# First images of both halves: the second skip and the transform along w one cycle later, and half 0's output banks emptied by two engines

## The chip, the core and the metric

The kernel runs on one core of a Trainium2 chip. The core has five engines with queues of their own, each in order: PE (TensorE, matrix products), DVE (VectorE), ACT (ScalarE), POOL (GpSimd) and SP (SyncE, which only issues DMAs here). POOL and ACT issue DMAs too. Matmul results go to PSUM, eight banks of 128 partitions x 512 fp32. The metric is device time in microseconds of one execution: 2630.17 before the change, the median of three runs (2627.25 to 2636.5).

## The reference, cut to what matters

Two layers work on an image x of 256 x 256 points with 128 channels. Layer 0 is a gated attention along the rows, added to x. Layer 1 is a spectral block on the 256 images (tokens) of 256 x 128 points into which its input is cut. Its last part, to which the change belongs, reads in the reference:

```python
h0 = instance_norm(attn, norm2_w, norm2_b)
h1 = fno_layer(h0, mix_wr[0], mix_wi[0], ..., norm=True, act=True)
h2 = fno_layer(h1, mix_wr[1], mix_wi[1], ..., norm=True)
out = instance_norm(h2, mon_w, mon_b) + attn
```

An fno_layer adds a "skip" (a product with a 4 x 4 matrix over groups of four channels) to a spectral convolution (Fourier modes, mixed, and turned back into an image), the latter normed; the first of the two has a GELU behind it.

## The kernel before, in words

All times below are microseconds from the start of the span. Layer 0 ends at about 1450. Layer 1 handles its 256 tokens as two halves of 128 (one token per partition), half 0 and half 1, each image in 16 blocks of 2048 pixels. h1 of half 0, later of half 1, lies in SBUF in the tile `blocks`; `hb[b]` is its block b. The stages at the end follow each other like this:

1. `first_images(0, ...)`, 1964 to 2098: makes h1 of half 0, block by block, and the Fourier transform of h1 along w, written to `Yd`.
2. 2098 to 2241: the last blocks of y (attn before its norm) of half 1, the second modes of half 0 and the first modes of half 1.
3. `first_images(1, ...)` woven with `output_0`, 2241 to 2440: h1 of half 1 block by block, while half 0's output image h2 is made and written.
4. 2440 to the end: the second modes of half 1 and its output (`LastModes`, `Output1`).

**first_images** (L1695) runs a loop over cycles b = 0 to 16. One cycle of the old code puts on the queues:

- the loads of block b+1 on SP (`load`, L1701: four DMAs of 64 KB for the modes `gs`; in half 1 also two of 512 KB for `y`), and in half 0 the loads of the old image `xw` (`load_w`, L1711, two of 512 KB);
- first skip of block b into four PSUM banks `ups` (L1387, 32x32 tiles of PE, sixteen at a time), then `image` (L1372, tiles of 32x128) into the same banks, then four GELUs on ACT from the banks to `hb[b]` (L1750);
- in half 0, `add_w(b+1)` (L1719): ACT scales the raw block b+1 into the tile `w0` (L1727), POOL adds `xw` to it (L1730) and issues the write to `wd` (L1731). Blocks that were summed in an earlier stage are left out: 0, 1, half of 2, and 9 to 11;
- for block b-1: sixteen transposes on PE into four banks `htps` (L1762), copied to the tiles `hT` by DVE (L1774, and L1765 for the last, which ACT copies in half 1);
- here the loop yields 0, and in half 1 the caller puts in one step of `output_0`;
- for block b-1: second skip into four banks `sps` (L1387), of which DVE takes statistics (`bn_stats`, L1782); the product along w of the four `hT` into one bank `psA` (L1785), copied by ACT to `yA` (L1787) and written to `Yd` by a DMA from POOL's queue (L1788);
- the loop yields 1, and in half 1 the caller puts in the next step of `output_0`.

Buffers that set the order: `ups` (and `h2ps` of output_0) rotate over one set of four banks, `htps`, `sps` and `psA` over another set of four. `hT` has four tiles, `yA` two, `gs` of the first images two, `w0` three. `xw` for the second half of a block has one tile (L1715), so its load for the next block waits until POOL has added it.

**output_0** (L2088) calls `output` (L2072) for each block of half 0. The first step puts a skip (L1387) and an image (L1372) into four banks `h2ps` and has ACT empty all four into `hb[b]` (L2079). The second step has DVE add the result to `w` (L2085) and POOL issue the writes to the output (L2086). Its loads (`wd` 1024 KB at L2094, `gs` 4 x 64 KB) go to SP one block ahead. In half 1, block b's GELUs write over `hb[b]`, which output_0 must have added by then.

The queues of these stages are written out by hand: each engine executes in the order in which the program gives it its instructions.

Of the kernel before, what the change touches and what calls it, by code (L numbers as in the profile page):

```python
# [10 lines left out]
FP = mybir.dt.float32  # L11
AF = mybir.ActivationFunctionType
ALU = mybir.AluOpType
# [5 lines left out]
P = 128  # L19
# [681 lines left out]
def layer1(tc, I, C, ident, x1d, upool, U, Q2, groups, out):  # L701
# [6 lines left out]
    nc = tc.nc  # L708
    NT, H, W = 256, 256, 128
    L = lambda n: I["L1_conv_" + n]  # L710
    with ExitStack() as ctx:
# [86 lines left out]
        wp = gctx.enter_context(tc.tile_pool(name="wp", bufs=3))  # L798
# [35 lines left out]
        with tc.manual_schedule(engines=COMPUTE):  # L834
# [292 lines left out]
            ps = psa.tile([P, 512], FP, tag="a", name="gtps")  # L1127
# [9 lines left out]
            bfwd = load_const(late, "bfwd")  # L1137
# [4 lines left out]
            for t in range(2):  # L1142
                for b in range(2):
                    ps = psa.tile([P, 512], FP, tag="a", name=f"fvps_{t}_{b}")
# [49 lines left out]
        wp = hctx.enter_context(tc.tile_pool(name="wp2", bufs=2))  # L1194
# [86 lines left out]
        with tc.manual_schedule(engines=COMPUTE):  # L1281
# [25 lines left out]
            for sc in range(2):  # L1307
                nc.vector.tensor_scalar(mpT[:, sc, :], mT[:, sc, :], acol[:, sc, 0:1], None, ALU.mult)
                d = mpT[:, sc, sc * P : (sc + 1) * P]
# [5 lines left out]
            ps = psa.tile([P, 512], FP, tag="a", name="mbps")  # L1315
# [20 lines left out]
            for c in range(4):  # L1336
                ps = psa.tile([P, 512], FP, tag="a", name=f"fyps_{c}")
# [20 lines left out]
        hb = [blocks[:, b, :] for b in range(16)]  # L1358

        def by_turn(t):  # L1360

            return t.rearrange("p (n j w) -> p j n w", j=4, w=W)

        def rows_of(ps):
            return ps.rearrange("p (n w) -> p n w", w=W)
# [11 lines left out]
        def skip(ps, src, blk, stop):  # L1377


            parts = src if isinstance(src, list) else [src]  # L1380
            for k, part in enumerate(parts):
                n = slice(k * 4 // len(parts), (k + 1) * 4 // len(parts))
                for j in range(4):
                    for i in range(4):
                        r, o = slice(32 * i, 32 * i + 32), slice(32 * (i ^ j), 32 * (i ^ j) + 32)
                        w = blk[r, r] if len(blk.shape) == 2 else blk[r, j]
                        nc.tensor.matmul(rows_of(ps[j][o, :])[:, n], w, part[r, j], start=(k == 0), stop=stop)  # L1387
# [32 lines left out]
        hstat = sp.tile([P, 64, 6], FP, name="hstat")  # L1420
# [274 lines left out]
        def first_images(a, wp, yp, psk, pst, first=None):  # L1695


            h = halves[a]
            ys, gss = {}, {}

            def load(b):  # L1701
                if a == 1:
                    ys[b] = []
                    for k in (2 * b, 2 * b + 1):
                        pool, tag, bufs = (wp, "wx", 1) if k % 3 == 0 else (yp, "yt", 2)
                        ys[b].append(pool.tile([P, HB], FP, tag=tag, name=f"y2_{k}", bufs=bufs))
                        nc.sync.dma_start(ys[b][-1], ydv[:, a, k * HB : (k + 1) * HB])
                gss[b] = wp.tile([P, 4, P], FP, tag="gs2", name=f"gs2_{a}_{b}")
                load_modes(gss[b], h.Gd1, b)

            def load_w(b):  # L1711
                for s in range(2):
                    if 2 * b + s in h.summed:
                        continue
                    t = (yp, "yt", 2) if s == 0 else (wp, "xw", 1)  # L1715
                    ys[b, s] = t[0].tile([P, HB], FP, tag=t[1], name=f"xw_{b}_{s}", bufs=t[2])
                    nc.sync.dma_start(ys[b, s], x1v[:, a, b * NB + s * HB : b * NB + (s + 1) * HB])

            def add_w(b):  # L1719

                todo = [s for s in range(2) if (b, s) in ys]
                if not todo:
                    return
                t = yp.tile([P, NB], FP, tag="xt", name=f"w0_{b}", bufs=3)
                for s in todo:
                    px = slice(s * HB, (s + 1) * HB)
                    nc.scalar.activation(t[:, px], hb[b][:, px], AF.Identity, scale=h.col[:, 3:4])  # L1727
                for s in todo:
                    px = slice(s * HB, (s + 1) * HB)
                    nc.gpsimd.tensor_tensor(t[:, px], t[:, px], ys.pop((b, s)), ALU.add)  # L1730
                    nc.gpsimd.dma_start(wd[:, b * NB + s * HB : b * NB + (s + 1) * HB], t[:, px])  # L1731

            if first is None:
                load(0)
            else:
                ys[0], gss[0] = first
            if a == 0:
                load_w(0)
                add_w(0)
            for b in range(17):  # L1740
                if b < 15:
                    load(b + 1)
                    if a == 0:
                        load_w(b + 1)
                if b < 16:
                    ps = [psk.tile(f"ups_{a}_{b}_{j}") for j in range(4)]
                    skip(ps, [by_turn(y) for y in ys.pop(b)] if a else by_turn(hb[b]), h.bl0, False)
                    image(ps, gss.pop(b), bs4)
                    for j in range(4):
                        nc.scalar.activation(  # L1750
                            by_turn(hb[b])[:, j], rows_of(ps[j]), AF.Gelu,
                            bias=h.turn[:, 2 * j + 1 : 2 * j + 2], scale=h.turn[:, 2 * j : 2 * j + 1],
                        )
                    if a == 0 and b < 15:
                        add_w(b + 1)
                if b > 0:
                    turned = by_turn(hb[b - 1])
                    hT = {}
                    for j in (1, 2, 3, 0):
                        ps = pst.tile(f"htps_{a}_{b}_{j}")  # L1760
                        for n in range(4):
                            nc.tensor.transpose(ps[:, n * P : (n + 1) * P], turned[:, j, n, :], ident)  # L1762
                        t = hT[j] = wp.tile([P, 512], FP, tag="hT", name=f"hT_{a}_{b}_{j}", bufs=4)
                        if j == 0:
                            (nc.scalar.copy if a else nc.vector.tensor_copy)(t, ps)  # L1765
                            continue
                        v = t.rearrange("p (n c d x) -> p n c d x", n=4, c=2, d=2)
                        if j == 1:
                            v = v[:, :, :, ::-1].rearrange("p n c d x -> p (n c) d x")
                        elif j == 2:  # L1770
                            v = t.rearrange("p (n c x) -> p n c x", n=4, c=2)[:, :, ::-1]
                        else:
                            v = t.rearrange("p (n c x) -> p n c x", n=4, c=4)[:, :, ::-1]
                        nc.vector.tensor_copy(  # L1774
                            v, ps.rearrange("p (m c x) -> p m c x", m=v.shape[1], c=v.shape[2])
                        )
                yield 0
                if b > 0:
                    ps = [pst.tile(f"sps_{a}_{b}_{j}") for j in range(4)]
                    skip(ps, turned, blk[1], True)  # L1780
                    for j in range(4):
                        nc.vector.bn_stats(hstat[:, 4 * (b - 1) + j, :], ps[j])  # L1782
                    psA = pst.tile(f"psA_{a}_{b}")
                    for j in (1, 2, 3, 0):
                        nc.tensor.matmul(psA[32 * j : 32 * j + 32, :], bfwd, hT[j], start=True, stop=True)  # L1785
                    yA = wp.tile([P, 512], FP, tag="yA", name=f"yA_{a}_{b}")
                    nc.scalar.copy(yA, psA)  # L1787
                    (nc.scalar if a and b == 16 else nc.gpsimd).dma_start(  # L1788
                        h.Yd[16 * (b - 1) : 16 * b].rearrange("(n j) f t -> (j f) n t", j=4),
                        yA.rearrange("f (n t) -> f n t", n=4),  # L1790
                    )
                yield 1

        def turned_blocks(h):
# [277 lines left out]
        def output(a, b, gs, w, psk):  # L2072

            krs, c0 = (halves[a].col[:, k : k + 1] for k in (14, 9))
            ps = [psk.tile(f"h2ps_{a}_{b}_{j}") for j in range(4)]
            skip(ps, by_turn(hb[b]), by_blocks(halves[a].bl0), False)
            image(ps, gs, bs4)
            for j in range(4):
                nc.scalar.activation(  # L2079
                    by_turn(hb[b])[:, j], rows_of(ps[j]), AF.Identity, bias=c0, scale=krs  # L2080
                )
            yield
            for s in range(2):
                px = slice(b * NB + s * HB, b * NB + (s + 1) * HB)
                nc.vector.tensor_tensor(w[s], w[s], hb[b][:, s * HB : (s + 1) * HB], ALU.add)  # L2085
                nc.gpsimd.dma_start(outv[:, a, px], w[s])  # L2086
# [307 lines left out]
```

## Time and profile before

| what | value |
|---|---|
| time, median of three runs | 2630.17 us (2627.25 to 2636.5) |
| profiled execution, its own time | 2637.42 us |
| span of that execution | 2635.7 us |
| PE busy in the span | 2418.5 us (92%) |
| DVE, ACT, POOL busy | 2024.6, 1422.7, 1476.0 us |
| first images of half 0, from the first skip to the last psA | 1963.9 to 2098.3 |
| first images of half 1 with output_0, from the first h2ps to yA of block 15 | 2241.2 to 2439.8 |
| GELU from a bank, ACT (L1750), one | 777 ns |
| emptying an h2ps bank, ACT (L2079), one | 776 ns |
| copy of a bank to hT, DVE (L1774), one | 685 ns |
| bn_stats of a bank, DVE (L1782), one | 686 ns |
| add of xw, POOL (L1730), one | 2370 ns |

In a timeline row the first two numbers are the start and the length of a run of like instructions; the ends of matmuls are modelled, and consecutive ones overlap a little, so the distance between two starts is the better measure of PE's time. In a table by windows, the last three columns are PE's granted clock (1.00 is full), the mean busy share of the 16 DMA engines, and what they moved. A busy share a little over 1 means saturated.

### The profile page before, as it was taken

What the parts mean: (1) busy time and instruction counts of PE and PEld (TensorE: products, weight loads), DVE (VectorE), ACT (ScalarE), POOL (GpSimd) and SP (SyncE); (2) the same over time, 40 slices, a digit from 0 to 9 for tenths busy, and PEclk for the clock granted to TensorE, in tenths of its full rate; (3) what the DMA queues carried; (4) which work ended last, traced back from release to release, by engine and by line L of the source; (5) the groups of instructions that cost most, each with busy time, mean ns of one, the idle gap of its engine ahead of it and who ended that gap; (6) DMA issues with size and microseconds to landing.
All of it is one profiled execution on the core that took longest, in us unless ns stands there. A gap on an engine that the chain in (4) does not pass through costs nothing. (4 is left out here: it accounts for less than half of the span.)

```text
span 2635.7 us, 88777 instructions
## 1 busy us (share of the span) xinstructions
PE 2418.5 (92%) x37590; PEld 1546.8 (59%) x37590; DVE 2024.6 (77%) x2872; ACT 1422.7 (54%) x2732; POOL 1476.0 (56%) x1043
## 2 busy tenths in 40 slices
PE   6899999999999999999998999998979978899754
PEld 5555556565556555656554567786754556455633
DVE  7799999999999999999997457567645645465455
ACT  0377888888888888888885122001016401565232
POOL 1299999999999999999995012002136411111011
PEclk9999999999999999999999999999989988899855
DMA  9755565666656565665653011788877764998699
GB/s 364 217 101 102 102 109 103 106 106 108 105 103 108 102 109 102 109 104 105 108 104 65 5 59 65 264 272 291 296 276 260 238 239 140 316 361 312 195 377 349
DMA packets 1016549, 458.49 MB, mean 174 GB/s; under 512 B 831062, under 2 KB 946729, under 8 KB 1009752
## 3 DMA queue, kind: packets, MB, share of 16 engines
q1 hardware_dynamic: 980120, 364.71, 55.0%
q0 software_dynamic: 22832, 81.54, 8.0%
q10 hardware_dynamic: 13200, 6.56, 0.9%
q8 instruction: 298, 4.88, 0.8%
q14 instruction: 99, 0.81, 0.1%
HBM read 317.36 MB, written 135.27 MB: 172 GB/s over the span
## 5 line engine op out<-in xcount | busy, mean ns | idle before, releaser
L422 POOL TENSOR_TENSOR e<-e,b1T 128x1024 f32<-128x1024 f32 x255 | 604.8, 2372 | 82.6 <-ACT e L404 82.0
L427 POOL TENSOR_TENSOR es<-e 128x512 f32<-128x512 f32 x512 | 648.9, 1289 | 0.1
L449 DVE RECIPROCAL av<-av 128x256 f32<-128x256 f32 x256 | 452.2, 1766 | 9.1
L404 ACT ACTIVATE sc<-sc,b2T 128x512 f32<-128x512 f32 x514 | 340.0, 662 | 122.4 <-PE sc L395 109.9
L404 ACT ACTIVATE e<-sc,b2T 128x512 f32<-128x512 f32 x510 | 323.4, 694 | 0.0
L420 DVE TENSOR_TENSOR e<-sc,b1T 128x1024 f32<-128x1024 f32 x257 | 312.3, 1215 | 7.1 <-ACT sc L404 3.6
L395 PE MATMUL sc<-qkT 32*128 32x256 f32 x4096 | 294.9, 401 | 1.2 <-DVE e L420 1.2
L1505 PE MATMUL yps<-xt,mpT 128*128 128x256 f32 x1024 | 249.1, 394 | 30.8 <-DMA xt<-x1d 15.0
L437 PE MATMUL av<-e,v 128*32 128x256 f32 x4096 | 268.7, 379 | 1.8 <-DVE gate L450 1.7
L395 PEld LDWEIGHTS sc<-qkT 32*128 32x128 f32 x4096 | 185.7, 184 | 113.4 <-issue 52.7
L1505 PEld LDWEIGHTS yps<-xt,mpT 128*128 128x128 f32 x1024 | 193.6, 194 | 75.7 <-DVE yt L1517 20.0
L437 PEld LDWEIGHTS av<-e,v 128*32 128x32 f32 x4096 | 130.1, 109 | 125.9 <-issue 38.5
L1521 POOL DMA_DIRECT2D yd<-yt x32 | 17.5, 546 | 324.6 <-DVE yt L1517 322.1
L367 ACT ACTIVATE qkT<-qk,qb 128x512 f32<-128x512 f32 x256 | 174.4, 681 | 3.2 <-PE qk L337 3.2
L337 PE MATMUL qk<-turned,wT_wk 128*32 128x256 f32 x2048 | 164.5, 393 | 0.4 <-DVE g_ve L35 0.4
L494 ACT ACTIVATE turned<-turned 128x256 f32<-128x256 f32 x256 | 104.4, 409 | 111.7 <-DVE x1b L462 109.4
L337 PEld LDWEIGHTS u<-adft,x 128*32 128x32 f32 x4096 | 118.5, 110 | 74.9 <-issue 74.7
L442 PE MATMUL av<-es,ones 128*32 128x256 f32 x2048 | 160.7, 379 | 1.5 <-POOL es L427 1.5
L2079 ACT ACTIVATE blocks<-h2ps,col 128x512 f32<-128x512 f32 x128 | 88.9, 779 | 130.4 <-PE h2ps L1372 130.4
L345 DVE STREAM_TRANSPOSE turned<-xk 128x1024 f32<-128x1024 f32 x128 | 158.1, 1235 | 0.4 <-DMA xk<-in_L_conv_kv_x_dram 0.4
L337 PE MATMUL qk<-turned,wn_wq 128*32 128x256 f32 x2048 | 157.9, 380 | 0.0
L2086 POOL DMA_DIRECT2D out_dram<-w x64 | 34.3, 536 | 186.6 <-DVE w L2085 186.4
(566 smaller groups left out, 4266.0 us busy)
## 6 DMA issues: line engine op xcount, KB each, us to landing
xt<-x1d SPq DMA_DIRECT2D x128, 512.0 KB, 7.2
U<-in_x_dram SPq DMA_DIRECT2D x32, 1024.0 KB, 10.3
xk<-in_x_dram SPq DMA_DIRECT2D x512, 64.0 KB, 3.0
xk<-in_L_conv_kv_x_dram SPq DMA_DIRECT2D x512, 64.0 KB, 2.6
x1d<-x1b SPq DMA_DIRECT2D x512, 64.0 KB, 2.2
out_dram<-w POOLq DMA_DIRECT2D x64, 512.0 KB, 7.9
x<-x1d SPq DMA_DIRECT2D x126, 256.0 KB, 3.4
y<-yd SPq DMA_DIRECT2D x62, 512.0 KB, 8.8
```

The costliest lines, as they stand in the source:

```text
L337: nc.tensor.matmul(out[hd], w[:, hd], src, start=start, stop=stop)
L345: nc.vector.transpose(turned[:, a : b + 1 : b - a].rearrange("p k (b c) -> p k b c", c=32), t)
L367: nc.scalar.activation(r["qkT"], ps, AF.Identity, bias=self.qb)
L395: nc.tensor.matmul(sc[h // 2][:, h % 2, c * 256 : (c + 1) * 256], qkT[p, 256 + c * P : 256 + (c + 1) * P], qkT[p, 0:256], start=True, stop ...
L404: nc.scalar.activation(r["e"][1][:, :, c, :] if hp and s < NS - 1 else z, z, AF.Exp, bias=b2T[:, c, s : s + 1])
L420: nc.vector.tensor_tensor(e, sc.rearrange("p h x -> p (h x)"), w, ALU.mult)
L422: nc.gpsimd.tensor_tensor(e, e, w, ALU.mult)
L427: nc.gpsimd.tensor_tensor(es, e[:, :, 0, :], e[:, :, 1, :], ALU.add)
L437: nc.tensor.matmul(ps[hd, 0:256], p["v"][:, 2 * (s % 2) + c, hd], r["e"][h // 2][:, h % 2, c, :], start=(c == 0), stop=(c == 1),)
L442: nc.tensor.matmul(ps[32 * h : 32 * h + 32, 256:512], self.ones, r["es"][h // 2][:, h % 2, :], start=True, stop=True,)
L449: nc.vector.reciprocal(rd, rd)
L1505: nc.tensor.matmul(rows_of(ps[j]), mpT[:, sc, tt], by_turn(xt[:, sc])[:, j], start=(sc == 0), stop=False,)
```

## The change

The loop of `first_images` goes over 18 cycles in place of 17, and its parts become small functions. Transposes of block b-1 stay in cycle b; the second skip (with its statistics) and the product along w (with its write) handle block b-2.

- In half 0 a cycle now gives PE: first skip of b, second skip of b-2, image of b, product along w of b-2, transposes of b-1. The two skips are one run of 32x32 tiles.
- In half 1 the second skip of b-2 comes first, then the first skip of b. The skip of output_0, put in at the yield, is not next to it in PE's queue: its image lies between.
- ACT's four GELUs are split: banks 0 and 1, then the copy `yA` of block b-2, then banks 2 and 3. In half 0 `add_w(b+1)` comes behind the transposes in program order, so on ACT it still follows the GELUs.
- At the end, the product along w of block 15 comes before the second skip of block 15.
- In `output` of half 0, DVE empties banks 2 and 3 of `h2ps` with a tensor_scalar; ACT empties 0 and 1.
- On POOL's and SP's queues half 0 keeps its order: the write of `Yd` of block b-1 still follows the adds of block b+1. In half 1 the write of `Yd` comes one output block later in POOL's queue.

The core of the diff:

```diff
-            for b in range(17):
+            for b in range(18):
                 if b < 15:
                     load(b + 1)
                     if a == 0:
                         load_w(b + 1)
+                if a and 1 < b < 17:
+                    second_skip(b - 2)
                 if b < 16:
-                    ps = [psk.tile(f"ups_{a}_{b}_{j}") for j in range(4)]
-                    skip(ps, [by_turn(y) for y in ys.pop(b)] if a else by_turn(hb[b]), h.bl0, False)
+                    ps = first_skip(b)
+                if not a and 1 < b < 17:
+                    second_skip(b - 2)
+                if b < 16:
                     image(ps, gss.pop(b), bs4)
...
+                    gelu(b, ps, (0, 1))
+                if b > 1:
+                    along_w(b - 2)
+                if b < 16:
+                    gelu(b, ps, (2, 3))
+                if 0 < b < 17:
+                    turn_back(b - 1)
+                if a == 0 and b < 15:
+                    add_w(b + 1)
                 yield 0
...
+                if b == 17:
+                    second_skip(15)
                 yield 1
...
             for j in range(4):
-                nc.scalar.activation(
-                    by_turn(hb[b])[:, j], rows_of(ps[j]), AF.Identity, bias=c0, scale=krs
-                )
+                if a == 0 and j > 1:
+                    nc.vector.tensor_scalar(by_turn(hb[b])[:, j], rows_of(ps[j]), krs, c0, ALU.mult, ALU.add)
+                else:
+                    nc.scalar.activation(
+                        by_turn(hb[b])[:, j], rows_of(ps[j]), AF.Identity, bias=c0, scale=krs
+                    )
```

`second_skip`, `along_w`, `turn_back`, `first_skip` and `gelu` hold the old statements unchanged, apart from the block index.

More of the change, by code (lines that the diff above doesn't have):

```diff
@@ L1739, in first_images, with turn_back @@
                 add_w(0)
-            for b in range(17):
+            hTs = {}
+            def turn_back(b):
+                turned = by_turn(hb[b])
+                hT = hTs[b] = {}
+                for j in (1, 2, 3, 0):
+                    ps = pst.tile(f"htps_{a}_{b}_{j}")
+                    for n in range(4):
+                        nc.tensor.transpose(ps[:, n * P : (n + 1) * P], turned[:, j, n, :], ident)
+                    t = hT[j] = wp.tile([P, 512], FP, tag="hT", name=f"hT_{a}_{b}_{j}", bufs=4)
+                    if j == 0:
+                        (nc.scalar.copy if a else nc.vector.tensor_copy)(t, ps)
+                        continue
+                    v = t.rearrange("p (n c d x) -> p n c d x", n=4, c=2, d=2)
+                    if j == 1:
+                        v = v[:, :, :, ::-1].rearrange("p n c d x -> p (n c) d x")
+                    elif j == 2:
+                        v = t.rearrange("p (n c x) -> p n c x", n=4, c=2)[:, :, ::-1]
+                    else:
+                        v = t.rearrange("p (n c x) -> p n c x", n=4, c=4)[:, :, ::-1]
+                    nc.vector.tensor_copy(
+                        v, ps.rearrange("p (m c x) -> p m c x", m=v.shape[1], c=v.shape[2])
+                    )
@@ new lines, in second_skip, with along_w @@
+            def second_skip(b):
+                ps = [pst.tile(f"sps_{a}_{b}_{j}") for j in range(4)]
+                skip(ps, by_turn(hb[b]), blk[1], True)
+                for j in range(4):
+                    nc.vector.bn_stats(hstat[:, 4 * b + j, :], ps[j])
+            def along_w(b):
+                hT = hTs.pop(b)
+                psA = pst.tile(f"psA_{a}_{b}")
+                for j in (1, 2, 3, 0):
+                    nc.tensor.matmul(psA[32 * j : 32 * j + 32, :], bfwd, hT[j], start=True, stop=True)
+                yA = wp.tile([P, 512], FP, tag="yA", name=f"yA_{a}_{b}")
+                nc.scalar.copy(yA, psA)
+                (nc.scalar if a and b == 15 else nc.gpsimd).dma_start(
+                    h.Yd[16 * b : 16 * b + 16].rearrange("(n j) f t -> (j f) n t", j=4),
+                    yA.rearrange("f (n t) -> f n t", n=4),
+                )
@@ new lines, in first_skip, with gelu @@
+            def first_skip(b):
+                ps = [psk.tile(f"ups_{a}_{b}_{j}") for j in range(4)]
+                skip(ps, [by_turn(y) for y in ys.pop(b)] if a else by_turn(hb[b]), h.bl0, False)
+                return ps
+            def gelu(b, ps, js):
+                for j in js:
+                    nc.scalar.activation(
+                        by_turn(hb[b])[:, j], rows_of(ps[j]), AF.Gelu,
+                        bias=h.turn[:, 2 * j + 1 : 2 * j + 2], scale=h.turn[:, 2 * j : 2 * j + 1],
+                    )
@@ L1744, in first_images @@
                         load_w(b + 1)
+                if a and 1 < b < 17:
+                    second_skip(b - 2)
                 if b < 16:
-                    ps = [psk.tile(f"ups_{a}_{b}_{j}") for j in range(4)]
-                    skip(ps, [by_turn(y) for y in ys.pop(b)] if a else by_turn(hb[b]), h.bl0, False)
+                    ps = first_skip(b)
+                if not a and 1 < b < 17:
+                    second_skip(b - 2)
+                if b < 16:
                     image(ps, gss.pop(b), bs4)
-                    for j in range(4):
-                        nc.scalar.activation(
-                            by_turn(hb[b])[:, j], rows_of(ps[j]), AF.Gelu,
-                            bias=h.turn[:, 2 * j + 1 : 2 * j + 2], scale=h.turn[:, 2 * j : 2 * j + 1],
-                        )
@@ L1754, in first_images @@
[L1754 to L1776, printed above, removed]
@@ L1777, in first_images @@
-                yield 0
[L1778 to L1791, printed above, removed]
+                    gelu(b, ps, (0, 1))
@@ L2078, in output @@
             for j in range(4):
-                nc.scalar.activation(
-                    by_turn(hb[b])[:, j], rows_of(ps[j]), AF.Identity, bias=c0, scale=krs
-                )
+                if a == 0 and j > 1:
+                    nc.vector.tensor_scalar(by_turn(hb[b])[:, j], rows_of(ps[j]), krs, c0, ALU.mult, ALU.add)
+                else:
+                    nc.scalar.activation(
+                        by_turn(hb[b])[:, j], rows_of(ps[j]), AF.Identity, bias=c0, scale=krs
+                    )
             yield
```

## The prediction

> **What bounds the kernel now.** I read the slices of the page first: PE is busy nearly everywhere, but in the stages that the change touches so are the DMA engines. Then the runs on PE in order of time. A cycle of half 0's first images:
>
> ```profile
> 2017.95 1.16 PE L1387 MATMUL ups<-blocks,bl 32*32 32x512 f32 x32
> 2019.04 1.17 PE L1372 MATMUL ups<-k_bsyn,gs 32*128 32x128 f32 x32
> 2020.14 1.97 PE L1762 MATMUL htps<-ident,blocks 128*128 128x128 f32 x16
> 2022.04 2.40 PE L1387 MATMUL sps<-blocks,blk 32*32 32x512 f32 x32
> 2024.37 1.07 PE L1785 MATMUL psA<-hT,k_bfwd 128*32 128x512 f32 x8
> 2025.36 1.16 PE L1387 MATMUL ups<-blocks,bl 32*32 32x512 f32 x32
> ```
>
> By the distance of starts a skip costs 1.09, the image 1.10, transposes 1.90, psA 0.99. The second skip costs 2.33 where the same sixteen tiles cost 1.09: its banks come free only as DVE copies `htps` out. A cycle is 7.41, of which 1.24 is that wait. Third, the stage's chain of waits, where PE is not what carries the end:
>
> ```profile
> 2072.90 2.40 POOL w L1730
> 2075.31 6.68 DMA xw<-x1d
> 2082.13 2.36 POOL w L1730
> ...
> 2092.61 8.67 DMA Yd<-yA
> 2101.38 0.59 ACT yA L1787
> ...
> 2108.33 8.25 DMA xt<-x1d
> ```
>
> The one `xw` tile makes a loop: add, then the next load may be issued, it lands 4.3 to 7.2 later, add. Second adds of blocks 4 to 8 end at 2007.6, 2016.8, 2024.9, 2034.5, 2041.9: 8.6 a block, slower than PE's 7.41. The end goes the same way: last adds, write of Yd(13), yA(15), write of Yd(15), load of YT, and behind it in SP's queue the xt that PE waits for. Fourth, the windows of half 1's stage, with one of half 0's:
>
> ```profile
> core 0: us, PE busy (x) PEld busy (x) DVE busy (x) ACT busy (x) POOL busy (x), PEclk, DMA share, GB/s
> ...
> 2271.00:2283.00 12.00, 11.25 (x219) 5.61 (x212) 6.02 (x8) 7.70 (x12) 1.07 (x2) 1.00 0.91 302
> 2283.00:2293.50 10.50, 9.85 (x227) 5.51 (x226) 6.67 (x10) 6.63 (x10) 1.83 (x3) 1.00 1.01 358
> ...
> 2325.00:2335.70 10.70, 10.05 (x223) 5.89 (x224) 6.57 (x10) 6.64 (x10) 1.83 (x3) 1.00 1.03 371
> ...
> 2378.00:2393.00 15.00, 12.13 (x216) 7.95 (x216) 3.71 (x6) 6.47 (x10) 0.77 (x1) 0.77 0.80 266
> 2393.00:2404.00 11.00, 10.35 (x220) 5.61 (x216) 6.71 (x10) 6.63 (x11) 1.87 (x3) 1.00 0.83 291
> ```
>
> From 2283 to 2378 the DMA share is 1.00 to 1.03: nothing is left there, however PE is ordered. Only at the start, in the dip at 2378 and just behind it do the DMA engines have room.
>
> **Half 0, part by part.** *The later second skip* frees 1.24: DVE's four copies now lie beside the next first skip. PE's cycle is then 1.09+1.09+1.10+0.99+1.90 = 6.17. The longest load of another engine is ACT's 2.79+2.19+0.59 = 5.57. DVE has 8 x 0.62 = 5.0.
>
> *Where it goes.* SP issues gs(b) behind the xw load that waits for the second add of b-2. gs(9) landed 7.8 after that add (2034.47 to 2042.23) and PE did wait 0.42 for it; one quarter of gs(8) landed at 2032.65, and image 8 ran at 2033.86. So from block 8 on PE was already at this gate: running 1.24 a cycle faster up to block 7 only means waiting at 8 and 9. The loop itself starts earlier by at most 0.8 (second add of block 3 ends at 1999.4 in place of 2000.18: GELU 1.4 earlier, yA's 0.6 ahead of its second half). Blocks 9 to 11 have no adds; from image 9 to image 11 PE gains 2 x 1.24 = 2.5. The first scaled w of block 12 follows image 11's GELU: 0.8+2.5 = 3.3 earlier, less 0.6 for yA between the GELU pairs: 2.7. Behind it adds 12 to 15 run by POOL (2 x (2.37+0.30+0.57)+0.77+0.1 = 7.3 a block) and by the xw loop, unchanged, and so does the chain to xt. Gain 2.5, bounds 0 (loads land later, as they vary by 2.9) and 5.
>
> *Moved steps.* POOL's and SP's orders are the same, so no DMA is moved past another. *One run of two skips:* the Trainium skill (TensorEngine Tiling, "Key Properties") has changing the tiling mode drain PE. By the rule each merge saves a drain; by the rows a skip's two passes a tile need about the 0.99 of psA's two, so 1.09 holds at most 0.10 of it, 1.6 in 16 cycles, all behind DMA. I take 0; bound 1.6.
>
> **Half 1, part by part.** PE's cycle was 10.48: 1.09 (h2 skip)+1.10+1.09 (second skip)+0.99+1.43 (first skip, 64 pieces)+1.10+1.90 = 8.70, plus 1.0 in the h2 skip, waiting for ACT's GELUs, plus 0.65 in psA waiting for bn_stats.
>
> *DVE on banks 2 and 3.* No row shows this tensor_scalar; near are DVE's copy (0.69) and its TENSOR_SCALAR from a bank, D<-dps (0.75), against ACT's 0.78. I take 0.75. Two banks: 1.5 more on DVE, 6.7 to 8.2 a cycle, under 9.8. Behind it wait the adds to w, then bn_stats, then psA. The four banks are empty after about 1.5 in place of 2.8. ACT falls from 6.8 to 5.2.
>
> *The new cycle*, from the second skip's start: skips to 2.9 (first skip waits 0.5 for bank 1), image to 4.0; adds 1.6 to 3.95, first bn_stats 4.6, psA 4.7 to 5.7; yA 6.35, second GELU pair 7.75, transposes 7.6, h2 skip 8.7, image 9.8. So 9.8, and the extra wait for DVE is inside.
>
> *What is late next:* DMA. A full cycle moves y 2 x 512 KB, w 1024, out 2 x 512, gs 8 x 64, Yd 256: 3.93 MB, in 10.48 375 GB/s. Here a rule speaks against the change: the Trainium skill (DMA: Bandwidth & Descriptors, "Specifications") gives HBM about 358 GB/s per core, which makes 10.98 a cycle and leaves no gain. The trace has 386 from 2540 to 2620, so 10.2; rule and row leave 0 to 0.3 a cycle for cycles 2 to 9. I take 0 there. What remains:
> - Start: h2 banks empty 1.3 earlier, in cycle 1 no second skip and no psA (2.1+0.65). Up to 4 earlier at cycle 2; but only (1.03-0.91) x 12 = 1.4, and (1.03-0.81) x 12 = 2.6 from 2252 to 2264, of DMA time are idle. I take 2 (0 to 4).
> - The dip 2378 to 2393: idle DMA 0.23 x 15 = 3.4; half of it is PE restarting at clock 0.77. I take 1.5 (-2 to 3.5; faster PE may run dry more often).
> - Cycles 12 to 14, 10.93 each, because the GELU waits 2.40 for the add of its block: now that add ends at 3.95, beside skips and image. At 386 GB/s they'd be 0.7 shorter; the window 2404 to 2415 is full at 368. I take 1.5 in all (0 to 2.5).
> - End: product along w of block 15 no longer waits for its second skip (1.9), but for the last hT copies: 1.2 (0 to 2). The last statistics end about 0.9 later and delay the first half of f1ps; its second half waited 3.65 for YT, which covers that. Without that cover 0.9 is lost.
>
> Sum for half 1: 6.2. The two output blocks ahead of the stage wait for gs anyway (5.14): 0.
>
> **Sum.** 2.5+6.2 = 8.7. The profiled execution, 2637.42, would be 2628.7. It lies 7.2 over the median of the runs; I carry the same microseconds to the median: 2630.17-8.7 = 2621.5. What a measurement can tell from no change here is about 0.3%, 7.9 us: "faster" is below 2622.3.
>
> **The rivals.**
> - *DMA was only as late as PE let it be.* Then PE's cycles count: 16 x 1.24 = 20 in half 0, 14 x 0.68 = 9.5 in half 1, with the end 1.2: 31 off, 2599. For: PE has no gaps from 1988 to 2041. Against: share 0.88 and the 8.6 loop in half 0, 1.0 in half 1.
> - *DMA takes all of it.* Only blocks 9 to 11 give something: 2.5, 2627.7. For: windows at 1.03. Against: the idle shares at 2252, 2271, 2378 and 2393.
> - *Slower: yA in the middle of the GELUs.* yA waits for a Yd write of two blocks before; it waited 3.74 at 2041.63 and 7.62 at 2101.38 for DMA. Before, this delayed the next block; now it holds half a GELU, w of b+1 and so POOL's adds. It decides once Yd lands later than image and first GELU pair are done, about 10 after the second add; rows give 8.5. If it is so in the four cycles 6 to 9: 4 x 3.74 = 15 lost, less 6.2: 2639.
>
> **How the numbers follow.** Forecast 0.50 (own range 2616 to 2627; 0.3 beyond 0.3%), first rival 0.15, second 0.22, third 0.13. Faster 0.3+0.15 = 0.45; slower 0.12 (a little of the third is within); same 0.43. Range 2608 to 2633: part of the first rival and the worse half of the third stay out, about 0.2.
>
> **What would show it.** Right: sps runs of 1.1 in half 0; half 0 cycles of 6.2 only up to block 7 and for 10 and 11; PE waits for gs at blocks 7 to 9; second adds still 8 to 9 apart; half 1 cycles near 10.4 with share 1.0 and new waits of PE for y or gs; the stage between the halves about 2.5 earlier. Wrong: half 0's last add more than 5 earlier, half 1 cycles under 10, adds later than before, or ACT waiting for Yd between GELUs.

## The result, and the profile after

Twenty runs of each kernel on one chip: 2627.89 us after (2621.07 to 2643.06), 2631.8 before (2625.82 to 2648.52). The ratio is 0.9985, with a 95% interval of 0.9973 to 0.9996: 3.9 less (1.1 to 7.1), within the 0.3% that the forecast called no change. A later comparison of the same two kernels gave 0.9981 (0.9967 to 0.9995), by the ratio 5.0 less. The forecast was 8.7 less, just beyond that 0.3%. The profiled execution of after took 2625.89 (span 2624.1), 11.5 less than the profiled one of before; much of that is the spread of single executions.

Two stretches are compared below. **A** goes from the first ups to the first h2ps: half 0's first images and the stage behind them. **B** goes from the first h2ps to the second half of f1ps: half 1's first images with output_0, up to the first product that needs the late load of YT.

PE's runs in half 0, timeline of after, block 7 from its first skip to the product along w:

```profile
2018.39 1.45 PE L1387 MATMUL ups<-blocks,bl 32*32 32x512 f32 x32
2019.28 1.66 PE L1387 MATMUL sps<-blocks,blk 32*32 32x512 f32 x32
2020.94 0.48 PE L1372 MATMUL ups<-k_bsyn,gs 32*128 32x128 f32 x2
2023.39 1.58 PE L1372 MATMUL ups<-k_bsyn,gs 32*128 32x128 f32 x30 [1.96 <-DMA gs<-Gd]
2024.90 1.06 PE L1777 MATMUL psA<-hT,k_bfwd 128*32 128x512 f32 x8
```

Most of the wait in the second skip is gone (1.66 by the starts where it was 2.33; without a wait a skip takes 1.09), and a new one stands in the image: 1.96 for gs, which SP issues behind the xw load. The two skips together take about 2.6, not the 2.18 of the forecast.

Windows of half 1 in after (columns as before: busy times, then granted clock, DMA share, GB/s):

```profile
2269.40:2279.50 10.10, 10.07 (x232) 6.04 (x216) 8.10 (x12) 5.27 (x9) 1.83 (x3) 1.00 1.03 384
2313.00:2325.00 12.00, 10.64 (x233) 6.18 (x218) 8.74 (x13) 5.75 (x9) 1.83 (x3) 1.00 1.03 363
2325.00:2339.80 14.80, 12.70 (x231) 7.67 (x216) 7.90 (x12) 4.95 (x9) 1.83 (x3) 0.77 1.01 351
2388.80:2398.80 10.00, 9.34 (x232) 5.73 (x216) 8.10 (x12) 5.31 (x9) 1.83 (x3) 1.00 1.03 379
```

DVE is busier (8.1 a cycle, before 6.7), ACT less (5.3, before 6.6). A cycle that runs freely, in which PE waits for no load, takes 10.0. Others stretch with the DMA engines full, at full clock to 12.0; in the one of 14.8 PE's granted clock was 0.77 as well, and its sixteen transposes took 3.68 in place of 1.97. The end of half 1 in the chain of work, first before, then after:

```profile
2439.24 0.59 ACT yA L1787
...
2439.86 3.73 DMA Yd<-yA
...
2443.68 3.59 DMA YT<-Yd
...
2447.31 6.51 PE f1ps L1970 x128
```

```profile
2422.97 0.59 ACT yA L1779
...
2423.59 9.41 DMA Yd<-yA
...
2433.07 2.83 DMA YT<-Yd
...
2435.95 5.26 PE f1ps L2002 x128
```

yA(15) comes 9.2 earlier after the first h2ps, but its write takes 9.41 in place of 3.73. From yA(15) to the second half of f1ps it is 8.1 before and 13.0 after.

### The profile page after: what moved, and what is told of

It is laid out like the page before. It is cut to its first block, busy times and chain, and to the rows that moved or that the text cites. A ratio compares the mean times of both kernels' runs of the same rounds, so it can differ in the third digit from the quotient of the medians.

```text
span 2624.1 us, 88703 instructions
## 1 busy us (share of the span) xinstructions
PE 2403.4 (92%) x37590; PEld 1555.3 (59%) x37590; DVE 2048.4 (78%) x2904; ACT 1398.7 (53%) x2700; POOL 1474.5 (56%) x1043
## 5 line engine op out<-in xcount | busy, mean ns | idle before, releaser
L1794 ACT ACTIVATE blocks<-ups,turn 128x512 f32<-128x512 f32 x128 | 92.7, 781 | 100.4 <-PE ups L1372 61.0
```

## The experiments

All runs in one table; "before" is that kernel on the same chip.

| kernel | time | before | ratio (95%) | A | B |
|---|---|---|---|---|---|
| before, first profile | | | | 277.4 | 206.1 |
| after, first profile | 2627.89 | 2631.8 | 0.9985 (0.9973-0.9996) | 271.9 | 201.8 |
| e1_half0 | 2633.33 | 2635.0 | 0.9993 (0.9971-1.0014) | 273.8 | 206.8 |
| e2_half1 | 2641.47 | 2635.0 | 1.0021 (1.0002-1.0041) | 276.4 | 207.3 |
| e3_dve | 2639.31 | 2635.0 | 1.0009 (0.9990-1.0029) | 273.8 | 204.8 |
| e4_before | 2638.25 | 2635.0 | 1.0013 (0.9992-1.0033) | 278.4 | 204.4 |
| e7_xw_after | 2617.82 | 2635.34 | 0.9933 (0.9911-0.9955) | 260.7 | 207.5 |
| e8_xw_before | 2632.57 | 2635.34 | 0.9980 (0.9968-0.9992) | 272.8 | 208.3 |
| e9_light_after | 2623.29 | 2635.34 | 0.9953 (0.9936-0.9970) | 270.6 | 192.2 |
| e10_light_before | 2629.87 | 2635.34 | 0.9973 (0.9959-0.9987) | 275.7 | 196.9 |
| e11_yt | 2616.20 | 2636.53 | 0.9931 (0.9902-0.9960) | 259.4 | 201.9 |
| e12_gelu | 2619.71 | 2636.53 | 0.9948 (0.9928-0.9968) | 260.0 | 202.6 |
| e13_after | 2630.55 | 2636.53 | 0.9981 (0.9967-0.9995) | 271.6 | 204.3 |
| e15_ya | 2631.12 | 2636.05 | 0.9988 (0.9972-1.0003) | 270.1 | 200.6 |

**The parts alone, and nothing.** The loop keeps a switch per half (`old = a == 1` in e1, `a == 0` in e2), which puts the second skip and the product along w back behind the first yield with index b-1; both leave the tensor_scalar out:

```diff
+            old = a == 1
+            for b in range(17 if old else 18):
...
+                if old and b > 0:
+                    second_skip(b - 1)
+                    along_w(b - 1)
```

> Only half 0 gets the new order; half 1 keeps the old one and ScalarE empties all its output banks. Two lengths are read from the trace: A, from the first ups to the first h2ps (277.4 in the profile of before, 271.9 after), and B, from the first h2ps to the second half of f1ps (206.1 before, 201.8 after). Theory 1 (each half saves a little that its own loop lets through, and loses some of it at its end): A 271 to 273, B 205 to 207, time 2 to 5 below before. Theory 2 (the gain is half 1's alone): A 276 to 278, time as before within 1.5. Theory 3 (the pair of profiles differs by chance of the transfers): A anywhere between 270 and 279 without regard to the order, time as before.

> Only half 1 gets the new order; half 0 keeps the old one and ScalarE empties all of half 0's output banks. Theory 1 (the DMA engines are full in half 1 and the end gives back 5 of the 9 gained before it): A as before, 276 to 278, B 202 to 205, time 1 to 4 below before; yA(15) about 8 after the first h2ps earlier than before, the write of Yd(15) lands 8 to 10 after its issue. Theory 2 (PE's order decides in half 1): B 199 to 201, time 5 to 7 below. Theory 3 (chance): B between 200 and 208, time as before.

e3 is before with the change's edit to `output` alone, e4 is before unchanged.

> The kernel before with only one edit: VectorE empties banks 2 and 3 of the h2 skip in place of ScalarE. Theory 1 (the 1.0 that PE waits in the h2 skip is hidden by full DMA engines, so it only shows where they have room): B 204 to 206, time 0 to 2 below before. Theory 2 (the emptying is the part of the change that gains): B 201 to 203, time 3 to 5 below. Rival against both: VectorE's two more instructions of about 0.7 stand ahead of the adds to w and of bn_stats, which hold psA; B 207 to 210, time 1 to 4 above before.

> The kernel before once more, unchanged: what the measurement makes of no change, and a second profile of it. Theories 1 and 2: time within 1.5 of before, A 276 to 279, B 205 to 207, with the hole of the DMA engines at the restart of PE's clock at about the same place. Theory 3 (chance decides between the pair): A or B differ from the first profile of before by 4 or more.

The times don't show what each part is worth: the unchanged kernel itself read 3 off (2638.25), with an interval 11 wide. Only e2's interval leaves out "no change", and on the other side: 5.5 more (0.5 to 10.8), where theory 1 said 1 to 4 less. In A the orders differ, touching at one end: 273.8 to 278.4 with half 0's old order and its xw loop (before, e2, e3, e4, e10; mean 276.3), 270.6 to 273.8 with the new one (after, e1, e9, e13; mean 272.0). That is 4.3 for half 0's order, from one profile a kernel; e1 alone lies 0.8 above theory 1's range in A. B spreads too widely for one profile each: e4 lies below what theory 1 gave it, e2 above it, e1 and e3 inside, and theory 3 is right that the pair of first profiles overstates B. e2's yA(15) comes 3.8 sooner than in before, not 8.

But cycles that run freely repeat to 0.1, and there the parts show. PE's timeline in e2 (new order, ACT empties all four banks), then in e9 below (new order, DVE empties two), the first skip and the image:

```profile
2349.18 3.30 PE L1387 MATMUL ups<-y,bl 32*32 32x256 f32 x64
2352.41 1.17 PE L1372 MATMUL ups<-k_bsyn,gs 32*128 32x128 f32 x32
```

```profile
2332.14 2.13 PE L1387 MATMUL ups<-y,bl 32*32 32x256 f32 x64
2334.20 1.17 PE L1372 MATMUL ups<-k_bsyn,gs 32*128 32x128 f32 x32
```

With ACT alone the first skip takes 3.23 by the starts, as it waits for the h2ps banks; with DVE's help 2.06. In the old order the same edit costs. psA in e3, then in e10, which lacks the edit:

```profile
2347.93 1.06 PE L1785 MATMUL psA<-hT,k_bfwd 128*32 128x512 f32 x8 [1.13 <-DVE hstat L1782]
```

```profile
2327.88 1.07 PE L1785 MATMUL psA<-hT,k_bfwd 128*32 128x512 f32 x8 [0.65 <-DVE hstat L1782]
```

Free cycles of half 1: 10.5 old, 11.0 old with the edit, 11.1 new without it, 10.0 new with it. By the cycle each part alone is slower; only both together are faster. The rival in e3's expectation, VectorE's instructions ahead of bn_stats, is right about the cycle (0.5), and not about B.

**What holds half 0.** Two tiles of xw; to make room, half 0's yA is taken from the ring of three that holds gs. e7 is after with this, e8 before with this:

```diff
-                    t = (yp, "yt", 2) if s == 0 else (wp, "xw", 1)
+                    t = (yp, "yt", 2) if s == 0 else (wp, "xw", 2)
...
-                yA = wp.tile([P, 512], FP, tag="yA", name=f"yA_{a}_{b}")
+                if a == 0:
+                    yA = yp.tile([P, 4, P], FP, tag="gs", name=f"yA_{a}_{b}", bufs=3)
+                    yA = yA.rearrange("f n t -> f (n t)")
+                else:
+                    yA = wp.tile([P, 512], FP, tag="yA", name=f"yA_{a}_{b}")
```

> The changed kernel with two tiles for xw in place of one (room for it is made by taking half 0's yA from the ring of three that holds gs). Theory 1 (in half 0 the loop of add, load, add holds the blocks, not PE): the second adds follow each other in 7.3 or less in place of 8.6, image 8 comes 3 or more earlier after the first ups, yA(14) and yA(15) wait for no write of Yd, A is 264 to 269 in place of 271.9 to 273.8, and the time is 3 to 8 below that of the changed kernel. Rival (loads are late because the DMA engines are busy, whatever tile they go to): A stays at 270 to 274.

> The kernel before with the same two tiles for xw and the same place for yA. Theory 1: A 270 to 274 in place of 273.8 to 278.4, so that the new order is worth 5 to 8 in A once the loop is gone, in place of some 3.6 with it. Rival (DMA engines): A stays at 274 to 278 and the difference between the orders stays at 3 to 4.

> The changed kernel with only the other half of the edit that made room: half 0's yA from the ring of three, and xw still one tile. It tells which of the two brought A from 271.9 down to 260.7. Theory 1 (the xw loop): A 269 to 272, stalls for gs at blocks 7 to 9 stay, and at most the 1 to 3 that yA(14) and yA(15) held at the end are won; time as the changed kernel within 3. Rival (two tiles of yA that wait for their writes): A 260 to 264, blocks 6.64 apart throughout, time 12 or more below the changed kernel.

e15 is after with only the yA part. e7 is 0.9933 of before, 17.5 less by the medians (five runs), and its interval lies clear of both kernels'. Idle time of POOL ahead of its adds of xw, in the view of that tile over 1985 to 2095, of after and then of e7 (releaser: us, times):

```profile
  ACT w L1727: 19.5, 2
  DMA xw<-x1d: 5.4, 4
  DMA gs<-Gd: 1.4, 1
```

```profile
  ACT w L1727: 19.5, 2
```

The waits for xw and gs are gone, second adds follow each other 7.3 apart, image 8 comes 3.4 sooner after the first ups, and PE's cycle is 6.6 to 6.7 from block 3 on (e8: 7.41). e8 less e7 is 12.1 in A, as much as 16 x 0.76: with the loop gone, half 0's order is worth about its whole PE time, and with the loop 4.3. (One profile each: the last yA comes 10.4 sooner, the last add 7.4, so that the two numbers meet is in part chance.) e8's A is the one theory 1 expected, but the orders differ by more than its 5 to 8; e7's A lies below its 264 to 269, and the time is some 13 below after, by the ratios to before, where 3 to 8 was expected: the loop cost more than I had thought. e15, where A is 270.1, shows that the room made for yA did not do it; the second tile of xw by itself wasn't run. e15's ACT waits differ from after's; over 1965 to 2110, of after and then of e15 (total, times, longest):

```profile
ACT yA L1779 <- DMA Yd<-yA: 12.4, 2, 6.4
```

```profile
ACT yA L1783 <- PE psA L1777: 6.7, 2, 3.6
```

yA(14) and yA(15) no longer wait for writes and yA(15) comes 6 sooner, but A is only 1.9 shorter, and in the time e15 can't be told from after.

**What holds half 1.** Both orders with less to write; seven eighths of half 0's output are left out:

```diff
+                n = HB if a else HB // 8
-                px = slice(b * NB + s * HB, b * NB + (s + 1) * HB)
+                px = slice(b * NB + s * HB, b * NB + s * HB + n)
...
-                nc.gpsimd.dma_start(outv[:, a, px], w[s])
+                nc.gpsimd.dma_start(outv[:, a, px], w[s][:, :n])
```

> The changed kernel, where the writes of half 0's output are cut to their first eighth of each tile (7/8 of that half's output is left out; every other instruction stays), so that a cycle of half 1 moves 3.0 MB in place of 3.9. Theory 1 (half 1 is held by the bandwidth of the DMA engines): cycles of 9.6 to 10.0 all through the stage, share 0.80 to 0.90, B 11 to 20 shorter than in the changed kernel. Theory 2 (PE's order or a chain of waits sets the cycle): B as before within 4.

> The kernel before with the same writes cut to an eighth (7/8 of half 0's output is left out). Theory 1: cycles of about 10.5, which is PE's own, B 3 to 10 shorter than in the kernel before, and 9 to 13 longer than in the changed kernel with the same cut: the 0.68 a cycle that the full DMA engines hid comes out. Theory 2: B as before within 4, and the difference between the two orders no larger than 4.

Starts of half 1's images after the first h2ps, worked out from the traces. Full writes are means: old order of before, e1, e4, e8; new order with the DVE edit of after, e7, e12, e13, e15.

| | block 2 | block 9 | block 15 | second half of f1ps (B) |
|---|---|---|---|---|
| full, old | 43.2 | 119.7 | 185.5 | 206.4 |
| full, new | 39.7 | 117.2 | 178.7 | 203.4 |
| light, old | 40.7 | 114.9 | 176.6 | 196.9 |
| light, new | 37.7 | 109.1 | 168.5 | 192.2 |

From block 2 to 9 the orders take 76.5 and 77.5 with full writes, 74.2 and 71.4 with light ones. So the new order is shorter by 2.8 where the DMA engines have room and by nothing where they are full: theory 1. With light writes that is one profile each, and with full ones single profiles spread from 74.0 to 80.6; but seven free cycles at 0.5 make 3.5. The windows of these seven cycles, of after, e13 and e9:

```profile
2271.90:2351.80 79.90, 72.93 (x1514) 43.93 (x1512) 56.84 (x78) 37.21 (x56) 12.71 (x21) 0.96 1.02 355
```

```profile
2278.30:2353.70 75.40, 67.98 (x1516) 40.64 (x1514) 57.32 (x78) 37.45 (x56) 12.81 (x21) 1.00 1.03 363
```

```profile
2273.30:2344.70 71.40, 67.07 (x1519) 40.30 (x1516) 57.42 (x79) 37.62 (x56) 12.97 (x22) 1.00 0.93 300
```

At 1.02 and 1.03 the engines moved 355 to 363 GB/s, with light writes 300 at 0.93. What SP waits for before it can issue loads shows the same; of after, then of e9, over these windows (total, times, longest):

```profile
SPq L1396 <- DMA y<-yd: 15.4, 9, 2.2
SPq L1396 <- DMA w<-wd: 14.2, 6, 3.1
SPq L1707 <- PE ups L1387: 4.7, 2, 3.0
```

```profile
SPq L1707 <- PE ups L1387: 22.1, 7, 4.4
SPq L1396 <- DMA y<-yd: 3.4, 3, 1.8
```

With full writes SP waits for earlier loads to land, with light ones for PE to use up y. In neither does it wait for a write of the output to free a tile of w, so half 1 isn't held by a loop through w as half 0 is by one through xw. B is 11.2 and 9.5 shorter than the means with full writes, and cycles are 10.0 and 10.5, as theory 1 expected; the share stayed above its 0.90 in e9. The part that failed is the size of the difference: e10's B is 4.7 above e9's, not 9 to 13. The free cycles differ by 0.5 instead of 0.68, and the end gives 3.4 of the 8.1 back.

**What the end gives back.** e11 is e7 with the early load of YT cut to the rows that need one write less; the late load grows from 32 to 48 rows:

```diff
-                for lo, hi in ((0, 96), (96, P)):
+                for lo, hi in ((0, 80), (80, P)):
```

> The changed kernel with two tiles for xw, and the early load of YT cut to rows 0 to 80, which need only the write of Yd(12), in place of 0 to 96. From yA(15) to the second half of f1ps it takes 8.1 to 10.4 in the five profiles with half 1's old order and 12.4 to 13.3 in the four with the new one. Theory 1 (the write of Yd(15) lies behind that early load in the DMA engines, since the new order issues it 7 after Yd(13) and not 12): with the early load some 10 sooner, 8 to 10 again, and the time 2 to 5 below that of the kernel with two xw tiles alone. Rival (the wait is for the last statistics, which now come 3 later, or the write is slow by itself): 12 to 13.5 as before.

The end in e11's chain:

```profile
2410.69 0.59 ACT yA L1783
...
2411.31 4.49 DMA Yd<-yA
...
2417.11 6.93 DMA YT<-Yd
...
2424.09 1.96 PE f1ps L2006 x64
```

The write of Yd(15) lands in 4.49; the larger late load then takes 6.93. The second half of f1ps starts before that last load has landed, and stops for it; PE's timeline:

```profile
2419.91 1.08 PE L2006 MATMUL f1ps<-YT,k_efwd 128*32 128x128 f32 x32 [1.95 <-DMA YT<-Yd]
2421.23 1.08 PE L2006 MATMUL f1ps<-YT,k_efwd 128*32 128x128 f32 x32 [0.24 <-DMA YT<-Yd]
2424.09 1.96 PE L2006 MATMUL f1ps<-YT,k_efwd 128*32 128x128 f32 x64 [1.77 <-DMA YT<-Yd]
```

From yA(15) to its start it is 9.2, against 11.9 to 13.3 in the seven profiles of half 1's new order with the early load of 96 rows; to its end 15.4, against 17.6 to 19.3 (e7: 19.3). Theory 1 holds: the write was late because the early load was ahead of it. The last statistics come as late as in the seven (the first product starts 3.57 after yA(15) in all eight), so the rival fails. The trace's 4 can't be told in the time (2616.2 beside 2617.82 on different chips); it is the lowest measured.

**The split GELUs, and the control.** e12 is e7 with half 0's four GELUs ahead of yA; e13 is after unchanged.

```diff
-                    gelu(b, ps, (0, 1))
+                    gelu(b, ps, (0, 1) if a else range(4))
...
-                if b < 16:
+                if a and b < 16:
                     gelu(b, ps, (2, 3))
```

> The changed kernel with two tiles for xw, and in half 0 all four GELUs of a block ahead of yA. Theory 1 (the two skips take 2.66 in place of 2.18 because the fourth bank waits for a GELU that yA has put back): half 0 cycles of 6.2 in place of 6.64, A shorter by 3 to 7. Rival A (with the loop gone PE is held by POOL's 6.5 a block or by the DMA engines): A shorter by less than 2. Rival B (psA's bank comes free 1.2 later and the transposes wait for it): A longer by 2 to 6.

> The changed kernel once more, unchanged. Theory 1 (half 1 runs at the pace of the DMA engines in either order, so that the 201.8 of B in its first profile was a lucky one): A 270 to 274, B 203 to 208, time 2 to 6 below the kernel before. Theory 2 (B's 4 are the order's own): B 200 to 203.

PE in half 0, e7 and then e12, two skips and the image:

```profile
2017.87 1.22 PE L1387 MATMUL ups<-blocks,bl 32*32 32x512 f32 x28
2018.75 0.59 PE L1387 MATMUL sps<-blocks,blk 32*32 32x512 f32 x1
2018.90 0.61 PE L1387 MATMUL ups<-blocks,bl 32*32 32x512 f32 x4
2018.94 1.65 PE L1387 MATMUL sps<-blocks,blk 32*32 32x512 f32 x31
2020.53 1.17 PE L1372 MATMUL ups<-k_bsyn,gs 32*128 32x128 f32 x32
```

```profile
2017.66 1.14 PE L1387 MATMUL ups<-blocks,bl 32*32 32x512 f32 x32
2018.54 1.47 PE L1387 MATMUL sps<-blocks,blk 32*32 32x512 f32 x32
2019.94 1.17 PE L1372 MATMUL ups<-k_bsyn,gs 32*128 32x128 f32 x32
```

In e7 the last tiles of the first skip run late, as the fourth bank waits for a GELU behind yA; in e12 they don't, and the skips take 2.28 in place of 2.66. The cycle is 6.40, where theory 1 said 6.2, and the last yA of half 0 comes 3.6 sooner. Yet A is only 0.7 shorter, where theory 1 said 3 to 7. That is rival A's number, but it isn't PE's cycle that is held: POOL's second adds still follow each other 7.3 apart, the last add comes only 1.5 sooner, and PE's waits for xt in the next stage grow from 3.8 to 6.4. e13 repeats after: A 271.6, B 204.3, 5.0 less than before, theory 1's numbers.

## Why the prediction was about right, and where it was not

- **Half 0, PE's cycle 7.41 to 6.17: too low.** It is 6.65. I had counted yA's 0.6 ahead of the second GELU pair in POOL's start, but not that the next first skip waits for the fourth bank. It didn't matter while gs and the xw loop held the blocks.
- **Half 0, gain of 2.5 through the xw loop: the mechanism holds (e7, e8, e15), the size was low.** Waits for gs stand at blocks 7, 8 and 9. In the profiled pair the last add comes 2.8 sooner after the first ups, as worked out; A over all profiles is 4.3 shorter, inside the bounds of 0 to 5. Where the rest is won, behind the last add, stays open.
- **One run of two skips, taken as 0:** no run shows a gain. In e12 the two take 2.28, not less than twice the 1.09 of one alone.
- **Half 1, cycles 2 to 9 give nothing: right** (76.5 and 77.5). Here the Trainium skill's rule (DMA: Bandwidth & Descriptors, "Specifications", about 358 GB/s per core) was nearer than the row I set against it: these cycles ran at 355 to 363 on average, and the 386 came from the output stage, with another mix of transfers. It is no ceiling, though: single cycles of after moved 379 and 384. Both had led to 0.
- **Half 1, start 2, dip and last cycles 3: 5 in all, measured 6.8** at block 15, 3.5 of it by block 2 and 4.3 behind block 9.
- **Half 1, the end, 1.2 gained: failed.** This is the step that made the sum too large. yA(15) does come sooner after the last image; but from image 15 to the second half of f1ps it is 20.9 in the old order and 24.7 in the new (means of the table), 3.8 lost in place of 1.2 won. I had costed the end from the wait for YT as it was (3.65), as if that were a fixed point that covers later work. It is the end of a chain of writes and loads that the change itself moves: Yd(13) and Yd(15) are issued 7 apart in place of 12, so the early load of YT, released by Yd(13), now lies just ahead of Yd(15) (e11).
- **The tensor_scalar at 0.75 on DVE:** the free cycle of 10.0 beside the forecast 9.8 fits it. That the edit is harmful without the new order I hadn't seen. (The parts I listed for the old cycle add up to 10.35, not 10.48; the forecast doesn't hang on it.)
- **Sum.** By A and B the profiles give 4.3 + 3.0 = 7.3 off, the forecast was 8.7. That they lie so near is luck in part: half 0 and the start, dip and last cycles of half 1 each gave 1.8 more than forecast, and the end 5.0 less. The times give 3.9 (1.1 to 7.1) and 5.0 (1.3 to 8.7). Whether the difference between 7 and 4 is chance stays open: starts of A spread from 1958.6 to 1972.7 over the profiles, before any changed line has run.
- **Rivals.** That PE's order decides (31 off) fails as long as the xw loop stands; e7 beside e8 shows that 12 of it are there to be had. That DMA takes all of it (2.5 off) has the right mechanism in half 1 and lies nearest in size. yA between the GELUs didn't come to wait for Yd until blocks 14 and 15, which have no GELUs behind them.

## What to carry to other kernels

When a wait of the busiest engine is removed, look for the loop that closes through a single buffer (here a load that may start only when the add before it is done): it decides how much of the gain passes, and a second tile may be worth more than the reorder. Two edits that each move work to where another engine is just free must be costed together; alone, each of these made the free cycle longer. At the end of a stage, draw the chain of writes and loads anew for the changed order, since a transfer that a cheaper loop releases earlier can land in front of the one that counts.

## What was not expected of the hardware

The same 256 KB write of Yd(15) took 3.73 to land in before and 9.41 in after. In before the early load of YT, 1.57 MB from another engine's queue, was issued 4.3 to 6.8 ahead of it, in after 0.4 to 1.9 ahead; in e11, where only 0.66 MB came shortly ahead (2.8), it took 4.49. Over all profiles it is 3.7 to 6.3 in the six with half 1's old order and 7.3 to 9.4 in the seven with the new one and the early load of 96 rows.

The DMA share is a coarse measure of room near 1: 355 GB/s went with 1.02, 300 GB/s (e9, with smaller writes) with 0.93, and 287 GB/s (e10) with 0.87.
